# A two-layer graph kernel: the folded value-output product in seven products of 256 cubed, row maxima taken from adj, layernorm sums of two batches on ScalarE, the bias row ahead of the flag

## The chip, the cores and the metric

The kernel runs on one core of a Trainium2 chip. The metric is the device time of one execution in microseconds (us). Three runs of the kernel before took 1082.97, 1084.35 and 1084.44 us; the median is 1084.35.

The engines have short names here, as in the profile: PE is TensorE's matrix multiply and PEld its weight load, DVE is VectorE, ACT is ScalarE, POOL is GpSimd, SP is SyncE, which here only issues transfers. Each engine runs its own list of instructions in order and waits on semaphores for the others.

## What is computed

There are 32 batches of 512 rows with 512 features. Each goes through two layers, both with a layernorm and relu ahead and an addition behind:

```python
h = jnp.maximum(_layernorm(x, axis=-1), 0.0)
x = x + einsum('bnd,do->bno', einsum('nm,bmd->bnd', adj, h), weight) + bias
h = jnp.maximum(_layernorm(x, axis=-1), 0.0)
q, k, v = h @ Wq + bq, h @ Wk + bk, h @ Wv + bv      # 8 heads of 64
scores = q k^T / 8 + (1.0 - adj)[None, None, :, :] * -1e9
x = x + softmax(scores) v @ Wo + bo
```

`adj` is a 512 x 512 matrix of reals between 0 and 1, not of zeros and ones. The term -1e9 (1 - adj) therefore outweighs the scores: in each row the largest adj takes the whole softmax, unless two of them lie too close. The kernel looks for that at run time. It finds the largest adj of each row and the gap to the second, bounds the scores by the sums of squares of Wq and Wk, counts the rows that some row points to, and forms a flag. If the flag says so, attention is a row look-up: out[n] = h[idx[n]] @ (Wv Wo) + (bv Wo + bo). This holds for the given data, and the run takes that path (`single_path`).

## The kernel before

**The opening** (lines 72 to 268) runs once, in an order written out by hand (`tc.manual_schedule`). It loads the weights, adj, the first batches of x, and then does these things on PE, in this order:

- transposes of `wv` into `wvT` (`turn`, L116), four 128 x 128 at a time, and between them the folded product `wvo` = wv x wo (L148): for each of four row blocks four matmuls of 512 columns. ACT copies each result out of PSUM into `wvo` (L167), permuting the columns.
- transposes of adj into `adjT` (L106), which ACT copies out (L110).
- the first matrix product of batch 0, `yT` = h x adjT (L225): four blocks of four matmuls of 512 columns, between which come small matmuls of the flag: `few` (L232), `many` (L218, L219), the bias row bv x Wo (L224) and the flag itself (L221).

DVE meanwhile forms the bias row's parts (`bias_part`, L133 and L135), the row maxima and where they stand (`peaks`, L128 and L129), the statistics of batch 0 and 1 (`Norm.stats`, BN_STATS L319 and aggregate L320; `power` L325 with POOL's L326; `offset` L329), sums of blocks of adjT, w0 and wvo (`sum_a`, `sum_b`, L287 to L305), the decision (L203 to L212), `cvo` (L259) and the flag as an integer (L255). ACT makes `mask` = -1e9 (1 - adj) in two passes a row block (`scale`, L121 and L122), applies the layernorm with relu (`Norm.relu`, L337), squares Wq and Wk (L200) and empties PSUM. All engines then read the flag from memory and branch (L270).

**The rest** (`single_path`) is a loop over batches that interleaves layer 0 of one batch with the preparation of the next and layer 1 of the one before. A matrix product of 512 cubed is done by `product` (L382): seven products of 256 cubed, each four matmuls of 256 columns, with sums of blocks prepared by DVE. The seven pieces have the names p1, p5, u2, c11, c22, c12, c21 and three PSUM banks: p1, u2, c22 and c21 add up in one bank, p5 and c12 in another. So u2 can only start when p1 has been copied out of the bank (L427 on ACT), and so on. Only batch 0's layer product is done in four row blocks with 512 columns (`layer0_rows`, L514).

What the other engines do beside the products is put into numbered steps: `put(batch, step, function)`. Steps 0 to 6 go beside layer 0 of batch b, 7 to 13 beside the aggregation of batch b + 1, 14 to 20 beside layer 1 of batch b - 1. For batch 0 the steps 0 to 3 go beside `layer0_rows` and hold steps 4 to 6 as well. Within a step each engine gets its instructions in the order of the `put` calls. In this first round stand, on DVE: the sums of batch 1's h (`h0_sum`), the additions L517, `number_rows`, the statistics of batch 0's second layernorm (`halves`), and those of batch 2's first (steps 8 to 11).

**The end.** The last batch's rows are gathered by GpSimd (`get_all`, L545), transposed on PE (`transpose_all`, L552) and multiplied with `wvo` (L564). Batch 30's rows are stored (`put_z`, L598), gathered again (`fetch`, L611), added (L616) and stored to the output.

Of the kernel before, what the change touches and what calls it, by code (L numbers as in the profile page):

```python
# [17 lines left out]
P = 128  # L18
# [7 lines left out]
def gnn_two_layers(ctx: ExitStack, tc: tile.TileContext, x, adj, w0, b0, wq, bq, wk, bk, wv, bv, wo, bo, out):  # L26
# [45 lines left out]
    with ExitStack() as tmp, tc.manual_schedule():  # L72
# [3 lines left out]
        adj_s, mask = (look.tile([P, C, N], F32, name=n) for n in ("adj_s", "mask"))  # L76
# [4 lines left out]
        wvT = yT  # L81

# [3 lines left out]
        for i, (t, w, c) in enumerate([(wv_s, wv, 0)] + [(wo_s, wo, c) for c in range(DC)] +  # L86
                                      [(wv_s, wv, c) for c in range(1, DC)]):
            (nc.sync, nc.scalar)[i % 2].dma_start(t[:, c:c + 1, :], rows(w, c, 1))
# [8 lines left out]
        for t, v in ((bv_c, bv), (bt[0], bq), (bt[1], bk)):  # L97
            nc.gpsimd.dma_start(t, v.rearrange("(c p) -> p c", p=P))
        first = look.tile([P, 1], F32, name="first")
        nc.scalar.activation(first, ones[:, 0:1], AF.Relu)  # L100

        def transposed(t, dst):
            pts = [ps_l.tile([P, C, P], F32, name=f"pt{m}") for m in range(C)]
            for c in range(C):
                for m in range(C):
                    nc.tensor.transpose(pts[m][:, c, :], t[:, c, m * P:(m + 1) * P], ident)  # L106
                if c % 2 == 1:
                    yield
            for m in range(C):
                nc.scalar.copy(dst[:, m, :], pts[m].rearrange("p c q -> p (c q)"))  # L110
            yield

        def turn(i):
            pt = ps_l.tile([P, C, P], F32, name=f"pt{i}")
            for j in range(DC):
                nc.tensor.transpose(pt[:, j, :], wv_s[:, i, j * P:(j + 1) * P], ident)  # L116
            (nc.scalar.copy, nc.scalar.copy, nc.vector.tensor_copy, nc.vector.tensor_copy)[i](
                wvT[:, :, i * P:(i + 1) * P], pt)

        def scale(c):  # L120
            nc.scalar.activation(mask[:, c, :], adj_s[:, c, :], AF.Copy, bias=-1.0)  # L121
            nc.scalar.activation(mask[:, c, :], mask[:, c, :], AF.Copy, scale=NEG)  # L122
# [4 lines left out]
        def peaks(c):  # L127
            nc.vector.max(top[:, c, :], mask[:, c, :])  # L128
            nc.vector.tensor_scalar(sel[:, c, :], mask[:, c, :], top[:, c, 0:1], None, op0=ALU.is_equal)  # L129
# [6 lines left out]

        flips = transposed(adj_s, adjT)
        idle = ps_l.tile([P, C, P], F32, name="pt3")
        for i in range(14):
            nc.tensor.transpose(idle[:, i % C, :], ident, ident)  # L140
        turn(0)
        later = {(0, 2): 1, (1, 0): 2, (1, 2): 3}
        for i in range(DC):
            ps = ps_l.tile([P, D], F32, name="mm", bufs=2)
            for j in range(DC):
                if (i, j) in later:
                    turn(later[i, j])
                nc.tensor.matmul(ps, wvT[:, j, i * P:(i + 1) * P], wo_s[:, j, :], start=(j == 0), stop=(j == DC - 1))  # L148
            if i == 0:
                for j in range(DC):  # L150
                    bias_part(j)
            if i == 1:
                next(flips)
                peaks(0)
                peaks(1)
            if i == 2:
                next(flips)
                for n in (0, 1):
                    norms[0].stats(n)
                norms[0].power()  # L160
                for v, r in ((b0, b0_r), (bo, cvo)):
                    nc.gpsimd.dma_start(r, bass.AP(tensor=v.tensor, offset=v.offset, ap=[[0, P], [1, D]]))
                norms[1].stats(0)
                norms[0].offset()
                norms[1].stats(1)
                norms[1].power()
            nc.scalar.copy(wvo[:, i, :].rearrange("p (c q e) -> p q c e", q=4, c=4),  # L167
                           ps.rearrange("p (q c e) -> p q c e", q=4, c=4))
            if i < 2:
                scale(2 * i)  # L170
                scale(2 * i + 1)
            if i == 2:
                next(flips)
                norms[0].relu(0)
                norms[0].relu(1)
                peaks(2)
                norms[1].offset()
                peaks(3)
                norms[1].relu(0)
                norms[1].relu(1)  # L180
# [3 lines left out]
        for c in range(2, C):  # L184
            nc.vector.tensor_add(both, both, sel[:, c, :])
        gap = look.tile([P, C], F32, name="gap")
        nc.vector.tensor_sub(gap, top[:, :, 0], top[:, :, 1])
        least = look.tile([P, 1], F32, name="least")
        nc.vector.tensor_reduce(least, gap, AX.X, ALU.min)
        for i in range(4):  # L190
            sum_b(nc, adjT_s, adjT, i)

        sums = look.tile([P, 4], F32, name="sums")
        few = ps_l.tile([P, 4, C], F32, name="few")
        many = ps_l.tile([P, 4, C], F32, name="many")
# [17 lines left out]

        for d in range(DC):
            ps = ps_l.tile([P, N], F32, name="mm", bufs=2)
            for m in range(C):
                if d == 2 and m == 1:
                    nc.tensor.matmul(many[:, 0, :], ones, used, start=True, stop=True)  # L218
                    nc.tensor.matmul(many[:, 1, :], ones, sums, start=True, stop=True)  # L219
                if d == 3 and m == 2:  # L220
                    nc.tensor.matmul(few[0:1, 1, 0:1], sure, ones[:, 0:1], start=True, stop=True)  # L221
                if d == 3 and m == 0:
# [761 lines left out]
```

## Time and profile before

| | us |
|---|---|
| median of three runs | 1084.35 |
| lowest, highest | 1082.97, 1084.44 |
| the profiled execution | 1083.92 |
| its span, first to last instruction | 1081.7 |
| PE busy in it | 1067.9 |
| opening, until the first product of `layer0_rows` | 43.57 |
| `layer0_rows`, to its end | 57.83 |

The span is what the profile covers; 2.2 us lie around it. TensorE's granted clock was 0.997. A line of the timeline has the start in us, the duration in us, the engine, the line of the code, the operation, what it writes and reads, and in brackets how long the engine had been idle before and what ended that. Consecutive instructions of one kind are drawn together as x4, x8; durations of neighbours overlap a little, so that work is best counted from start to start. In the lists of waits a line reads: who waited, for what, us in total, how often, the longest.

Some more starts from DVE's timeline: the peaks of the first row block at 15.92, the statistics of batch 0 from 18.16, the sums of adjT from 26.70, the statistics of batch 1 from 29.30, the flag at 39.98, the addition of the bias row to `cvo` at 42.64, the four additions of b0 from 44.68, the first sum of batch 1's h at 47.09.

### The profile page before, as it was taken

To read this page: it belongs to the slowest core of one execution; us is meant where nothing else is said; L and a number is where in the kernel's file an instruction comes from. 1 tells how busy PE (TensorE), PEld (TensorE's weight loads), DVE (VectorE), ACT (ScalarE), POOL (GpSimd) and SP (SyncE) were. 2 spreads that over 40 slices of the span, in tenths; PEclk is the share of its full clock that TensorE was granted. 3 is DMA by queue.
4 is the path that set the end of the run, shared out by engine and by line. 5 is a ranking of instruction groups with operands and counts; after the bars stand their busy time and mean duration, and the time that the engine had idled before them with its cause. 6 is when DMAs were issued, how large, how long until landed. Compare 5 with 4: busy or idle time off the path is not lost.

```text
span 1081.7 us, 15914 instructions
## 1 busy us (share of the span) xinstructions
PE 1067.9 (99%) x5418; PEld 941.9 (87%) x5418; DVE 902.8 (83%) x1851; ACT 362.2 (33%) x664; POOL 439.2 (41%) x522
## 2 busy tenths in 40 slices
PE   9999999999999999999999999999999999999996
PEld 5488989999998999998999998999898899999893
DVE  5888888888888888888888988888888888888873
ACT  5324323334422324432323432323332333442331
POOL 2024554333454333454433354433455434355413
PEclk9999999999999999999999999999999999999998
DMA  9144766667767666767666776665766666775638
GB/s 329 40 96 141 183 183 160 160 167 196 187 179 181 151 167 184 196 176 188 150 160 183 201 185 175 160 167 158 207 183 183 146 169 171 196 186 151 148 104 265
DMA packets 162443, 186.90 MB, mean 173 GB/s; under 512 B 15024, under 2 KB 102320, under 8 KB 162352
## 3 DMA queue, kind: packets, MB, share of 16 engines
q1 hardware_dynamic: 132816, 116.89, 37.2%
q0 software_dynamic: 27968, 66.61, 26.8%
q10 hardware_dynamic: 1568, 2.29, 0.6%
q8 instruction: 44, 0.72, 0.3%
q14 instruction: 47, 0.39, 0.1%
HBM read 96.28 MB, written 89.46 MB: 172 GB/s over the span
## 4 chain that ended last, share of the span: by engine, by line
PE 94%; DMA 2%; DVE 1%; POOL 1%; issue 1%; ACT 1%; SPq 0%; POOLq 0%; ACTq 0%; DVEq 0%
PE mm L388 89%; PE mm L148 1%; PE mm L225 1%; PE mm L514 1%; POOL x L602 1%; DMA yT<-z,place 0%; ACT h L337 0%; DMA h<-hs,idx 0%; DMA z<-zr 0%; DMA out_dram<-x 0%; PE pt L140 0%; DMA hs<-h 0%; PE pt L116 0%; DVE st L319 0%; DVE x L616 0%
## 5 line engine op out<-in xcount | busy, mean ns | idle before, releaser
L602 POOL DMA_INDIRECT x<-z,place x116 | 182.7, 1575 | 351.8 <-issue 193.7
L427 ACT COPY yT<-mm 128x512 f32<-128x512 f32 x124 | 71.8, 579 | 542.6 <-PE mm L388 534.6
L445 DVE TENSOR_TENSOR x<-mm,x 128x512 f32<-128x512 f32 x217 | 149.6, 689 | 86.1 <-PE mm L388 86.1
L337 ACT ACTIVATE h<-x,off,rstd 128x512 f32<-128x512 f32 x256 | 194.3, 807 | 52.2 <-DVE off L329 49.9
L326 POOL TENSOR_TENSOR rstd<-ve,mhalf 128x2 f32<-128x2 f32 (+1 forms) x97 | 106.3, 1095 | 233.5 <-DVE ve L325 233.0
L319 DVE BATCH_NORM_STATS2 st<-x 128x6 f32<-128x512 f32 x256 | 171.4, 670 | 1.2
L388 PE MATMUL mm<-adjT_s,h0s 128*128 128x256 f32 x744 | 170.8, 379 | 0.2 <-ACT yT L427 0.2
L388 PE MATMUL mm<-w_t,sel 128*128 128x256 f32 x744 | 170.7, 379 | 0.0
L388 PEld LDWEIGHTS mm<-adjT_s,h0s 128*128 128x128 f32 x744 | 141.2, 190 | 19.9 <-ACT yT L427 0.6
L388 PEld LDWEIGHTS mm<-w_t,sel 128*128 128x128 f32 x744 | 141.3, 190 | 19.3
L526 POOL DMA_INDIRECT hs<-h,dest x124 | 126.7, 1022 | 23.9 <-issue 22.4
L388 PE MATMUL mm<-w_s,yT 128*128 128x256 f32 x496 | 117.2, 379 | 0.0
L388 PE MATMUL mm<-adjT,h 128*128 128x256 f32 x496 | 117.2, 379 | 0.0
L388 PE MATMUL mm<-hTs,wvo_t 128*128 128x168 f32 x720 | 112.4, 306 | 0.0
L438 ACT ACTIVATE zs<-mm,cvo_c 128x168 f32<-128x168 f32 x240 | 83.0, 397 | 75.5 <-PE mm L388 75.5
L388 PEld LDWEIGHTS mm<-adjT,h 128*128 128x128 f32 x496 | 94.2, 190 | 13.2 <-issue 0.5
L388 PEld LDWEIGHTS mm<-hTs,wvo_t 128*128 128x128 f32 x720 | 105.5, 190 | 0.0
L388 PEld LDWEIGHTS mm<-w_s,yT 128*128 128x128 f32 x496 | 92.9, 190 | 11.3
L494 DVE TENSOR_TENSOR x<-x,b_r 128x512 f32<-128x512 f32 x124 | 83.8, 676 | 0.0
L388 PE MATMUL mm<-hT,wvo 128*128 128x168 f32 x480 | 78.2, 306 | 0.0
L388 PEld LDWEIGHTS mm<-hT,wvo 128*128 128x128 f32 x480 | 72.7, 190 | 1.6
L425 DVE TENSOR_TENSOR yT<-mm,yT 128x512 f32<-128x512 f32 x93 | 64.0, 688 | 5.7 <-PE mm L388 1.7
(159 smaller groups left out, 1285.7 us busy)
## 6 DMA issues: line engine op xcount, KB each, us to landing
out_dram<-x SPq DMA_DIRECT2D x124, 256.0 KB
x<-in_x_dram SPq DMA_DIRECT2D x120, 256.0 KB
hc<-hs SPq DMA_DIRECT2D x124, 176.0 KB
z<-zr SPq DMA_DIRECT2D x120, 96.0 KB
z<-zr SPq DMA_DIRECT2D x120, 80.0 KB
hs<-h,dest POOLq DMA_INDIRECT x124, 6.3
x<-z,place POOLq DMA_INDIRECT x116
adj_s<-in_adj_dram SPq DMA_DIRECT2D x2, 512.0 KB
```

Of the source, the lines that this page charges most:

```text
L148: nc.tensor.matmul(ps, wvT[:, j, i * P:(i + 1) * P], wo_s[:, j, :], start=(j == 0), stop=(j == DC - 1))
L319: self.nc.vector.bn_stats(st, self.src[:, self.chunks[i], :])
L326: self.nc.gpsimd.tensor_tensor(self.rstd, ve, self.mhalf[:, 0:n], ALU.pow)
L337: self.nc.scalar.activation(dst, src, AF.Relu, bias=self.off[:, i:i + 1], scale=self.rstd[:, i:i + 1])
L388: nc.tensor.matmul(bank[:, m, 0:half], lhs[:, k, m * P:(m + 1) * P], rhs[:, k, :], start=(first and m == 0 and k == 0), stop=(k == 1), ski ...
L425: nc.vector.tensor_add(dst, bank, dst)
L427: nc.scalar.copy(dst, bank)
L438: nc.scalar.activation(dst[:, m, :], bank[:, m, :], AF.Identity, bias=cvo_c[:, 2 * i + m:2 * i + m + 1])
L445: nc.vector.tensor_add(dst, bank, dst)
L494: nc.vector.tensor_add(X[b][:, c, :], X[b][:, c, :], b0_r)
L526: stored = nc.gpsimd.indirect_dma_start(out=HS[b], out_offset=bass.IndirectOffsetOnAxis(ap=dest[:, i:i + 1], axis=0), in_=H1[b][:, i, :], ...
L602: nc.gpsimd.indirect_dma_start(out=X[b][:, c, :], out_offset=None, in_=Z[b], in_offset=bass.IndirectOffsetOnAxis(ap=place[:, c:c + 1], axi ...
```

## The change

- The folded product is done as `product` does it, in seven products of 256 cubed (`fold`), with sums of blocks of wvT (in `xs[2]`, batch 2's room, as scratch) and of wo (in `wvo_t`, as scratch). The column permutation is now in how wo is read, in runs of 32 elements.
- The loads of wv and wo are cut otherwise: wv's first two row blocks in two column halves, the rest in halves of 512 KB. The rows b0 and bo are loaded at the start on POOL's queue.
- `mask` is gone; the maxima, the comparison and the index search use adj itself, and the first two values of each row are scaled afterwards (`tops`).
- The sums for the first layernorm of batches 1 and 2 are made on ACT, by a copy and a square that accumulate along the row (`NormAct`); batch 2's from steps 2 and 3 instead of 8 to 11.
- The bias row's parts are formed after the peaks; its matmul, and its addition to `cvo`, now come before the flag. Order on DVE around the flag changes with it; yT's last block is copied by ACT alone.
- Two sums of wvo go to batch 0's step 13, none is left in batch 1's step 5. `transpose_all(0)` of the last batch goes from step 18 to 19.

```diff
-        adj_s, mask = (look.tile([P, C, N], F32, name=n) for n in ("adj_s", "mask"))
+        adj_s = look.tile([P, C, N], F32, name="adj_s")
+        wvT_t = xs[2].rearrange("p c (a n) -> p c a n", a=2)
+        wo_t = wvo_t.rearrange("p t c (k n) -> p t c k n", k=2)
-        for i, (t, w, c) in enumerate([(wv_s, wv, 0)] + [(wo_s, wo, c) for c in range(DC)] +
-                                      [(wv_s, wv, c) for c in range(1, DC)]):
-            (nc.sync, nc.scalar)[i % 2].dma_start(t[:, c:c + 1, :], rows(w, c, 1))
+        for h in range(2):
+            nc.sync.dma_start(wv_s[:, 0:2, h * 256:(h + 1) * 256], rows(wv, 0, 2)[:, :, h * 256:(h + 1) * 256])
+            nc.scalar.dma_start(wo_s[:, 2 * h:2 * h + 2, :], rows(wo, 2 * h, 2))
+        nc.sync.dma_start(wv_s[:, 2:4, :], rows(wv, 2, 2))
...
+        for v, r in ((b0, b0_r), (bo, cvo)):
+            nc.gpsimd.dma_start(r, bass.AP(tensor=v.tensor, offset=v.offset, ap=[[0, P], [1, D]]))
...
-        def scale(c):
-            nc.scalar.activation(mask[:, c, :], adj_s[:, c, :], AF.Copy, bias=-1.0)
-            nc.scalar.activation(mask[:, c, :], mask[:, c, :], AF.Copy, scale=NEG)
+        def turn(i, j):
+            pt = corner(2 * i + j)
...
+            nc.scalar.copy(dst[:, 0, :], src[:, 0, :])
+            (nc.vector.tensor_copy if i == 0 and j == 0 else nc.scalar.copy)(dst[:, 1, :], src[:, 1, :])
+        def wo_sum(i):
+            t = [wo_t[:, n].rearrange("p c k (q e) -> p c (k q) e", e=32) for n in range(4)]
+            x1, x2 = ((wo_blk(0, 1), wo_blk(0, 0)), (wo_blk(1, 1), t[0]), (wo_blk(1, 1), wo_blk(0, 1)),
+                      (wo_blk(1, 0), t[1]))[i]
+            nc.vector.tensor_sub(t[i], x1, x2)
+        def fold(ps, lhs, rhs, first):
+            for m in range(2):
+                for k in range(2):
+                    r = rhs[:, :, k, :] if len(rhs.shape) == 4 and rhs.shape[2] == 2 else rhs[:, :, 4 * k:4 * k + 4, :]
...
+                    nc.tensor.matmul(o, lhs[:, k, m * P:(m + 1) * P], r,
+                                     start=(first and m == 0 and k == 0), stop=(k == 1), skip_group_check=True)
...
-            nc.vector.max(top[:, c, :], mask[:, c, :])
-            nc.vector.tensor_scalar(sel[:, c, :], mask[:, c, :], top[:, c, 0:1], None, op0=ALU.is_equal)
+            nc.vector.max(top[:, c, :], adj_s[:, c, :])
+            nc.vector.tensor_scalar(sel[:, c, :], adj_s[:, c, :], top[:, c, 0:1], None, op0=ALU.is_equal)
...
+        turn(0, 0)
+        wo_sum(0)
+        turn(0, 1)
+        u, v, w = (bank(i) for i in (0, 1, 2))
+        fold(u, blk(wvT, 0, 0), wo_blk(0, 0), True)
+        nc.scalar.copy(blk(wvo, 0, 0), u)
+        turn(1, 0)
+        turn(1, 1)
+        fold(w, blk(wvT, 1, 0), wo_blk(1, 0), True)
+        for i in range(1, 4):
+            wo_sum(i)
+        for i in range(3):
+            sum_a(nc, wvT_t, wvT, i)
+        nc.vector.tensor_add(blk(wvo, 0, 0), w, blk(wvo, 0, 0))
+        sum_a(nc, wvT_t, wvT, 3)
+        fold(v, wvT_t[:, 0], wo_t[:, 0], True)
+        nc.scalar.copy(blk(wvo, 1, 1), v)
+        fold(u, wvT_t[:, 1], wo_t[:, 1], False)
+        nc.scalar.copy(blk(wvo, 0, 1), u)
+        peaks(0)
...
+        next(flips)
+        fold(u, wvT_t[:, 2], wo_t[:, 2], False)
+        peaks(1)
+        norms[1].offset()
+        nc.vector.tensor_add(blk(wvo, 1, 1), u, blk(wvo, 1, 1))
+        next(flips)
+        next(flips)
+        fold(v, wvT_t[:, 3], wo_blk(1, 1), False)
...
+        peaks(2)
+        nc.vector.tensor_add(blk(wvo, 0, 1), v, blk(wvo, 0, 1))
+        fold(u, blk(wvT, 1, 1), wo_t[:, 3], False)
+        nc.scalar.copy(blk(wvo, 1, 0), u)
...
+        nc.vector.tensor_scalar(tops, top[:, :, 0:2], 1.0, NEG, op0=ALU.subtract, op1=ALU.mult)
...
+                if d == 2 and m == 3:
+                    nc.tensor.matmul(bias, ones, part, start=True, stop=True)
+                if d == 3 and m == 1:
                     nc.tensor.matmul(few[0:1, 1, 0:1], sure, ones[:, 0:1], start=True, stop=True)
...
-            nc.scalar.copy(yT[:, d, 0:N // 2 if d == 3 else N], ps[:, 0:N // 2 if d == 3 else N])
+            nc.scalar.copy(yT[:, d, :], ps)
...
+            if d == 1:
                 nc.vector.tensor_scalar_min(used, few[:, 0, :], 1.0)
                 if B > 1:
+                    norms.append(NormAct(nc, small, mhalf, xs[1], hs[1], range(C)))
+                    for c in range(C):
+                        norms[2].first(c)
...
             if d == 2:
                 decide()
+                if B > 1:
+                    norms[2].mean()
+                    for c in range(C):
+                        norms[2].second(c)
...
+                nc.vector.tensor_add(cvo, bias, cvo)
         nc.vector.tensor_copy(flag, few[0:1, 1, 0:1])
+        for i in range(2):
+            sum_a(nc, wvo_t, wvo, i)
+        if B > 1:
+            norms[2].power()
+        for c in range(C):
+            nc.vector.tensor_add(xs[0][:, c, :], xs[0][:, c, :], b0_r)
+        if B > 1:
+            norms[2].offset()
+            for c in range(C):
+                norms[2].relu(c)
+        for c in range(C):
+            nc.vector.max_index(idx[:, c, :], top[:, c, :], adj_s[:, c, :])
...
+class NormAct(Norm):
...
+    def row_sum(self, i, kind, to, **more):
+        c = self.chunks[i]
+        self.nc.scalar.activation(self.dst[:, c, :], self.src[:, c, :], kind, accum_out=to[:, i:i + 1], **more)
+    def first(self, i):
+        self.row_sum(i, AF.Copy, self.sum)
+    def mean(self):
+        self.nc.vector.tensor_scalar_mul(self.sum, self.sum, -1.0 / self.src.shape[2])
+    def second(self, i):
+        self.row_sum(i, AF.Square, self.sq, bias=self.sum[:, i:i + 1])
...
+            if b == 0:
+                put(2, 2, lambda b: ahead.append(ln0(b, NormAct)))
+                for c in range(C):
+                    put(2, 2, lambda b, c: ahead[0].first(c), c)
+                put(2, 3, lambda b: ahead[0].mean())
+                for c in range(C):
+                    put(2, 3, lambda b, c: ahead[0].second(c), c)
...
+                    put(0, 13, lambda b, i: sum_a(nc, wvo_t, wvo, i), i)
...
-                put(b, 18, lambda b: transpose_all(0))
+                put(b, 19, lambda b: transpose_all(0))
...
-                put(1, 5, lambda b: sum_a(nc, wvo_t, wvo, 3))
```

## The prediction

> **What bounds the kernel now.** I read the page's busy shares first, then the waits of TensorE (PE), then PE's timeline of the opening, then the other engines beside it.
>
> ```profile
> PE 1067.9 (99%) x5418; PEld 941.9 (87%) x5418; DVE 902.8 (83%) x1851; ACT 362.2 (33%) x664; POOL 439.2 (41%) x522
> ```
>
> PE is busy 1067.9 of 1081.7 us. The steady part, from 58 us on, is PE against PE; only a PE instruction removed or a PE wait removed can shorten the run. The waits of PE over the whole span:
>
> ```profile
> PE mm L514 <- DVE cvo L259: 1.7, 1, 1.7
> PE pt L140 <- POOL ident masks.py:199: 1.4, 1, 1.4
> PE pt L552 <- DMA h<-hs,idx: 1.4, 1, 1.4
> PE mm L148 <- ACT yT L117: 0.7, 1, 0.7
> ```
>
> So there is a wait at the hand-over from the opening to the first layer product (L514), and one near the end (L552). PE's timeline of the opening:
>
> ```profile
> 4.55 1.12 PE L116 MATMUL pt<-ident,x 128*128 128x128 f32 x4
> 6.34 3.78 PE L148 MATMUL mm<-x,yT 128*128 128x512 f32 x4 [0.68 <-ACT yT L117]
> ...
> 22.01 3.60 PE L148 MATMUL mm<-x,yT 128*128 128x512 f32 x8
> 25.45 3.60 PE L225 MATMUL mm<-adjT,h 128*128 128x512 f32 x8
> ...
> 43.57 7.10 PE L514 MATMUL mm<-w_s,yT 128*128 128x512 f32 x16 [1.72 <-DVE cvo L259]
> ...
> 57.83 1.89 PE L388 MATMUL mm<-adjT,h 128*128 128x256 f32 x8
> 59.55 3.62 PE L388 MATMUL mm<-adjT_s,h0s 128*128 128x256 f32 x16
> ```
>
> The timeline shows two records for one matmul. Four 512-wide ones take 25.45 - 22.01 = 3.44 us, 0.86 each; four 256-wide ones 59.55 - 57.83 = 1.72 us, 0.43 each. The first two 512-wide ones took twice that (x4 in 3.78, elsewhere 1.88). Beside them, what ScalarE (ACT) and VectorE (DVE) did where PE enters the steady part:
>
> ```profile
> 58.24 0.13 DVE L329 SCALAR_TENSOR_TENSOR off<-mv,rstd 128x2 f32<-128x2 f32 x1
> ...
> 58.54 1.52 ACT L337 ACTIVATE h<-x,off,rstd 128x512 f32<-128x512 f32 x2 [13.45 <-DVE off L329]
> 59.96 0.56 ACT L427 COPY yT<-mm 128x512 f32<-128x512 f32 x1
> ```
>
> This is the place that decides. The copy at 59.96 empties the first bank of `aggregate(1)` ("p1"), and the third product ("u2") adds into that bank. PE wanted u2 at 59.55 + 1.73 = 61.28; the copy ended at 60.52. The slack is 0.76 us, and behind it stands DVE, which delivers `off` last.
>
> **What the Trainium skill says.** "TensorE: Matmul & The Clock Gate", section "What's actually happening": PE runs at half clock until about 3.4 us of sustained work, and falls back after an idle window of that length. The trace agrees with the first half (records of twice the length until about 10.2 us); no gap here is long enough to show the second. "ScalarE: Activation LUTs", "Rules for kernel authors": about 0.3 us an ACTIVATE with a bias pointer and 0.83 ns an element. The trace has 0.81 us for 512 with two pointers (L337), 0.62 with none (L121). "DMA: Bandwidth & Descriptors", "Queues, rings and completion order": each DMA engine takes turns between its queues, packet by packet, so a load moved forward takes bandwidth from loads beside it. Here the DMA share is about 1.0 from 8 us on.
>
> **The change part by part**, against the profiled execution (1083.92 us, its span 1081.7 and 2.2 around it; the runs' median is 0.43 higher).
>
> *Folded product.* 16 x 0.86 = 13.76 us become 28 x 0.43 = 12.04 us: PE loses 1.72 us. Reading `wo` in runs of 32 elements I price at nothing: DVE L260, which walks the same way, takes 0.69 like any 512-wide pass. DVE gains 8 operand sums and 3 additions from PSUM at a start-to-start of 0.60 to 0.72 us (L299 to L305). Walk: transposes of the first corner end at 5.68 as before; ACT's half 0.37 and DVE's half 0.42 in turn, beside the second corner's transposes; first fold from 6.6, at half clock 4 x 0.85, to 10.0; eight transposes to 10.9; second fold to 12.65. ACT copies the last corner by 11.8, DVE's first sum is ready at 12.5, so the third fold runs 12.65 to 14.4 without a wait, the fourth to 16.1, adjacency transposes to 17.0, fifth fold to 18.7, transposes to 19.6, sixth to 21.3. DVE's list from 11.85: four sums and one addition to 15.0, peaks 1.12, statistics of batch 0 3.9 (18.16 to 22.06 before), peaks 1.13, `off`, then the addition that frees the last fold's bank, to 21.85. PE waits 0.6 us there and starts L225's products at 23.65, against 25.45: 1.8 us gained.
>
> *Bias row and flag.* The `bv` parts (2.85 us, 8.36 to 11.21 before) move on DVE to behind the peaks: DVE reaches `used` at 32.6, PE wants it at 32.2, a wait of 0.45. L225's part ends at about 40.0 (41.87 before). `cvo` is added ahead of the flag, so the hand-over waits only for ACT's full 0.58 us copy of yT: L514's products start at 40.7, against 43.57. Gained so far: 2.85 us. The two row loads now come first on POOL, which was idle from 4.1 to 20.2, 0.6 us each; their 0.5 MB at the 390 GB/s of the DMA view are at most 1.3 us for the weights beside them: 0 to +1.3, taken 0, since PE needs the last wv half only at 10.0.
>
> *Peaks from adj.* Eight ACT passes of 0.63 us go; none is on the path (DVE reached the peaks 0.24 us after the masks). One small DVE operation is added, 0.15.
>
> *Sums of batch 1 on ScalarE.* Four BN_STATS with aggregates (0.82 each, 3.3 us) leave DVE. ACT gets four sums between its yT copies, then four squares after the third copy: at (0.3 + 512 x 0.83 ns) = 0.72 us, an estimate from the ScalarE page and inside 0.62 to 0.81 of the trace, with an accumulator read of 0.09 start-to-start (L200) and an overlap of 0.09, 0.72 each. They run 37.0 to 39.9 and end as L225's part does: no PE cost. But `power` now waits on DVE for them, and behind it stand the four b0 additions (2.4), the row look-ups (2.7), the cvo column (1.3), then the whole list of the first layer product.
>
> *Sums of batch 2 on ScalarE.* DVE restarts at 39.9, has those 6.5 us, then h0 sums, additions, row numbering and statistics as before (47.09 to 58.24, 11.15 with a wait of 1.5 that falls away): `off` and `mean` at 56.2, against 58.24. So DVE gains 2.0 us where PE gained 2.85. ACT's four squares wait for `mean`, and they stand ahead of the two relus and the p1 copy: 56.45 + 4 x 0.72 + 1.42 + 0.56 = 61.3. PE has p1 and p5 done at 40.7 + 14.26 + 3.45 = 58.4 and waits 2.9 us for u2. u2 begins at 61.3, as before: **the opening's whole gain is handed back here, 0.0 us net** (+0.15 for wake-ups). Later the DVE list has caught up (it waits for PE at c11), so nothing more is owed.
>
> *Two wvo_t sums and the last one move* into batch 0's third product, where the products that need sel come 1.7 us apart: 0.
>
> *transpose_all one step later.* Before: the product ahead of it ended at 1054.0, PE waited for rows landing at 1055.4, transposed to 1056.03, then had two products of 1.14. Now one of these fills the wait: everything after is 1.14 us earlier, and the stores of batch 30 that the last gathers wait for as well. At worst the gathers are held by full DMA queues: 0 to 1.5, taken 1.14.
>
> Sum: 0.0 + 0.15 - 1.14 = -1.0 us: 1082.9, or 1083.3 from the median; I put **1082.9**.
>
> **The rivals.**
> (A) As summed; its own range 1081.6 to 1084.6, from squares at 0.62 to 0.81 (4 count after `mean`, 4 before `power`: 8 x 0.1) and the loads' 0 to 1.3.
> (B) The opening's gain survives: DVE reaches `mean` 2 us earlier than my list, because PE warms sooner or the passes pack closer, or ACT clears p1 sooner. For it: the DVE list is a sum of sixty steps. Against: every step's pitch is from the trace. 1083.92 - 1.14 - (1 to 2.85) = 1079.9 to 1081.8, centre 1081.0.
> (C) The wait before u2 grows until the clock falls. Place: PE between p5 and u2. At 0.72 the gap is 2.9 us; with 0.86 or more for a square it passes 3.4 us, and some 3.5 us of matmuls then run at half clock, +1.75 on top of 8 x 0.14 = 1.1, together 1084.8; with 1.0 each, 1086.9. So it is slower from 0.86. For it: the passes write, square, point at a bias and accumulate at once. Against: L200 squares and accumulates at 0.85 ns an element.
> (D) The loads decide: the bias rows delay wv, adj and x by the full 1.3 us and the DVE list with them: 1084.2.
> (E) It isn't what it says: the strided operand halves PE's rate in 12 matmuls, 12 x 0.43 = 5.2 us, part of it before the DVE list: 1087.
>
> **How the numbers follow.** A 0.42, B 0.31, C 0.15, D 0.09, E 0.03. A measurement of this kernel tells about 0.2%, 2.2 us, from no change: below 1082.2 is faster, above 1086.5 slower. Faster: B and 0.06 of A, 0.37. Slower: 0.10 of C and E, 0.13. Same: 0.50. The range 1080.3 to 1086.3 leaves out some 0.06 of B below and 0.13 above.
>
> **What would show it.** L225's product from about 23.6 and the first layer product from about 40.7: the fold and the flag are right. A PE wait of about 2.9 us for the ScalarE copy before u2: the handing back is right; its absence is B. Squares of 0.7 us; records of double length after that gap are C. First-fold records of more than 0.43 us past 12 us are E. At the end PE's wait for rows down from 1.4 to about 0.4. I am wrong if u2 begins before 60 or after 63 us.

## The result, and the profile after

The changed kernel takes 1088.96 us (median of five runs, 1088.29 to 1089.82), the kernel before, on the same chip, 1084.05 (1082.93 to 1084.44): ratio 1.0048, 95% interval [1.0033, 1.0062]. It is slower by about 4.9 us, where 1082.9 was predicted with a range to 1086.3. The profiled execution has a span of 1086.5 us, before 1081.7, at nearly the same granted clock (0.998, before 0.997).

The busy times of the page after:

```profile
PE 1067.3 (98%) x5442; PEld 946.3 (87%) x5442; DVE 901.4 (83%) x1847; ACT 369.8 (34%) x693; POOL 447.0 (41%) x522
```

TensorE (PE) is busy 0.6 us less than before in a span 4.8 us longer. So the new arithmetic, taken together, is not dear; PE waits more. Its list of waits after (who waited, for what, us in total, times, longest):

```profile
PE mm L459 <- ACT yT L498: 2.9, 1, 2.9
PE pt L128 <- DMA x<-in_L_gnn_Wv_dram: 1.5, 3, 0.8
PE pt L172 <- POOL ident masks.py:199: 1.4, 1, 1.4
PE mm L459 <- DVE zs L506: 1.3, 1, 1.3
PE mm L459 <- DVE x L516: 0.9, 1, 0.9
PE mm L585 <- ACT yT L272: 0.7, 1, 0.7
```

Four of these are new: 2.9 for ScalarE's copy of p1, 1.5 for wv's loads, 0.9 for an addition on VectorE (DVE), 1.3 for `zs`. Two are shorter: the hand-over to the first layer product (L585, before L514) waits 0.7 instead of 1.7, and the wait of 1.4 for rows near the end is down to 0.3. PE's timeline of the opening after:

```profile
5.16 1.11 PE L128 MATMUL pt<-ident,x 128*128 128x128 f32 x4 [0.48 <-DMA x<-in_L_gnn_Wv_dram]
7.04 1.11 PE L128 MATMUL pt<-ident,x 128*128 128x128 f32 x4 [0.77 <-DMA x<-in_L_gnn_Wv_dram]
7.95 3.13 PE L152 MATMUL mm<-x,yT 128*128 128x256 f32 x8
11.33 1.09 PE L128 MATMUL pt<-ident,x 128*128 128x128 f32 x8 [0.25 <-DMA x<-in_L_gnn_Wv_dram]
12.26 1.89 PE L152 MATMUL mm<-x,yT 128*128 128x256 f32 x8
...
25.19 5.31 PE L269 MATMUL mm<-adjT,h 128*128 128x512 f32 x12
...
42.78 7.11 PE L585 MATMUL mm<-w_s,yT 128*128 128x512 f32 x16 [0.72 <-ACT yT L272]
```

Three times PE waits for a piece of wv. The first fold starts at 7.95, where 6.6 was walked and the kernel before started its product at 6.34; the first two waits, 0.48 and 0.77, make most of that delay. The operation with adjT (L269, L225 before) starts at 25.19 against 25.45, the first layer product at 42.78 against 43.57: of the 2.85 us expected by then, 0.8 are there. The place where PE enters the steady part, all engines, after:

```profile
57.03 1.89 PE L459 MATMUL mm<-adjT,h 128*128 128x256 f32 x8
58.52 0.16 DVE L398 TENSOR_SCALAR sum<-sum 128x4 f32<-128x4 f32 x1
58.72 0.72 ACT L392 ACTIVATE h<-x,sum 128x512 f32<-128x512 f32 x1 [8.73 <-DVE sum L398]
...
61.56 1.50 ACT L380 ACTIVATE h<-x,off,rstd 128x512 f32<-128x512 f32 x2
62.97 1.04 ACT L498 COPY yT<-mm 128x512 f32<-128x512 f32 x2
63.58 0.70 PE L459 MATMUL mm<-adjT_s,h0s 128*128 128x256 f32 x2 [2.93 <-ACT yT L498]
```

`mean` is formed at 58.52; ScalarE, idle for 8.73 us, makes its four squares in 2.84 us, then two relus, then copies p1 out at 62.97; u2 (the line at 63.58) starts 2.3 us later than before (61.28). Two more starts complete the account: the first piece of layer 0's product is at 72.32 for batch 1 (69.92 before, 2.4 late) and at 107.18 for batch 2 (102.60, 4.6 late); the waits of 0.9 and 1.3 lie between. From there to 1044.6 us (last product with hT, 4.45 late) nothing changes.

### The profile page after: what moved, and what is told of

Read it like the earlier page. It is cut to its first block, busy times and chain, and to the rows that moved or that the text cites. A ratio compares the mean times of both kernels' runs of the same rounds, so it can differ in the third digit from the quotient of the medians.

```text
span 1086.5 us, 15990 instructions
## 1 busy us (share of the span) xinstructions
PE 1067.3 (98%) x5442; PEld 946.3 (87%) x5442; DVE 901.4 (83%) x1847; ACT 369.8 (34%) x693; POOL 447.0 (41%) x522
## 4 chain that ended last, share of the span: by engine, by line
PE 86%; DVE 6%; DMA 3%; POOL 1%; ACT 1%; issue 1%; SPq 1%; POOLq 0%; DVEq 0%; ACTq 0%
PE mm L459 86%; POOL x L673 1%; DMA x<-in_L_gnn_Wv_dram 1%; ACT h L392 1%; DMA yT<-z,place 1%; DVE st L362 1%; DMA z<-zr 1%; ACT h L380 0%; SPq L669 0%; DMA out_dram<-x 0%; DVE x L565 0%; DVE zr L664 0%; DVE yT L496 0%; DMA hc<-hs 0%; POOL rstd L369 0%
## 5 line engine op out<-in xcount | busy, mean ns | idle before, releaser
L516 DVE TENSOR_TENSOR x<-mm,x 128x512 f32<-128x512 f32 x217 | 149.8, 690 | 86.9 <-PE mm L459 86.9
L369 POOL TENSOR_TENSOR rstd<-ve,mhalf 128x2 f32<-128x2 f32 (+1 forms) x95 | 105.0, 1105 | 215.2 <-DVE ve L368 215.2
L362 DVE BATCH_NORM_STATS2 st<-x 128x6 f32<-128x512 f32 x248 | 166.1, 670 | 1.2
L597 POOL DMA_INDIRECT hs<-h,dest x124 | 133.0, 1073 | 25.6 <-issue 22.0
L459 PEld LDWEIGHTS mm<-w_s,yT 128*128 128x128 f32 x496 | 92.9, 190 | 11.3
L496 DVE TENSOR_TENSOR yT<-mm,yT 128x512 f32<-128x512 f32 x93 | 64.0, 688 | 12.1 <-PE mm L459 7.1
```

Source lines behind the costliest of these rows:

```text
L362: self.nc.vector.bn_stats(st, self.src[:, self.chunks[i], :])
L369: self.nc.gpsimd.tensor_tensor(self.rstd, ve, self.mhalf[:, 0:n], ALU.pow)
L459: nc.tensor.matmul(bank[:, m, 0:half], lhs[:, k, m * P:(m + 1) * P], rhs[:, k, :], start=(first and m == 0 and k == 0), stop=(k == 1), ski ...
L496: nc.vector.tensor_add(dst, bank, dst)
L516: nc.vector.tensor_add(dst, bank, dst)
L597: stored = nc.gpsimd.indirect_dma_start(out=HS[b], out_offset=bass.IndirectOffsetOnAxis(ap=dest[:, i:i + 1], axis=0), in_=H1[b][:, i, :], ...
```

## The experiments

The columns are the median, the number of runs and the ratio to the kernel before on the same chip, whose median was 1083.5 to 1083.8. Where two runs on different chips are compared, the ratios are the fairer measure: 0.0010 is 1.08 us.

| run | us | runs | ratio, 95% interval |
|---|---|---|---|
| e1: after, transposes at step 18 again | 1090.41 | 6 | 1.0056 [1.0044, 1.0068] |
| e2: after, batch 2's sums on DVE again | 1085.52 | 19 | 1.0016 [1.0009, 1.0023] |
| e3: after, batch 2's sums a step earlier | 1085.91 | 18 | 1.0018 [1.0011, 1.0025] |
| e4: after, wvo_t sums in batch 1 | 1086.39 | 10 | 1.0028 [1.0019, 1.0037] |
| e5: after, bias rows late | 1087.14 | 6 | 1.0031 [1.0019, 1.0043] |
| e15: after, GpSimd's five loads held back | 1086.79 | 22 | 1.0023 [1.0015, 1.0031] |
| e8: e3 and e4 | 1085.23 | 14 | 1.0015 [1.0005, 1.0025] |
| e7: e8, transposes at step 18 | 1085.63 | 22 | 1.0016 [1.0008, 1.0023] |
| e9: e8, bias rows late | 1083.00 | 22 | 0.9997 [0.9990, 1.0003] |
| e10: e8, GpSimd's five loads held back | 1082.56 | 22 | 0.9989 [0.9982, 0.9997] |
| e11: e10, last halves of wv and wo split | 1081.69 | 11 | 0.9985 [0.9975, 0.9995] |
| e6: before, transposes at step 19 | 1082.88 | 13 | 0.9986 [0.9978, 0.9995] |
| e13: before, bias rows first | 1084.05 | 14 | 1.0003 [0.9993, 1.0013] |
| e14: before, bq's and bk's loads held back | 1083.34 | 14 | 0.9997 [0.9988, 1.0006] |

### The wait before u2

```diff
 e2_dve_sums
-            if b == 0:
-                put(2, 2, lambda b: ahead.append(ln0(b, NormAct)))
...
+            put(b + 2, 8, lambda b: ahead.append(ln0(b)))
+            for c, step in enumerate((9, 10, 13, 13) if b > 0 else (8, 9, 10, 11)):
+                put(b + 2, step, lambda b, c: ahead[0].stats(c), c)
 e3_mean_early (and put ahead of what step 1 and 2 held)
-                    put(2, 2, lambda b, c: ahead[0].first(c), c)
+                    put(2, 1, lambda b, c: ahead[0].first(c), c)
-                put(2, 3, lambda b: ahead[0].mean())
+                put(2, 2, lambda b: ahead[0].mean())
...
-                    put(2, 3, lambda b, c: ahead[0].second(c), c)
+                    put(2, 2, lambda b, c: ahead[0].second(c), c)
```

> The changed kernel with batch 2's first layernorm sums on VectorE again, in steps 8 to 11. Theory Q (the four squares that stand ahead of the p1 copy on ScalarE hold PE): PE's wait of 2.9 us before the third product of the first aggregation shrinks to 0.3 or less, and the run to about 1086.2. Rival L (the late loads have put VectorE's whole list behind, the squares are only in its shadow): the wait stays above 2 us, the run at about 1088.5 or more.

> The changed kernel with batch 2's sums still on ScalarE, but the mean ahead of step 2 on VectorE, so that the squares run where ScalarE sat idle for 8.7 us. Theory Q: the wait before the third product goes to 0.3 or less as in the kernel with the sums on VectorE, about 1086.1. Rival L: the wait stays above 2 us. If this gains nothing while the kernel with the sums on VectorE gains, ScalarE's added work as such costs, not its place.

Both take the wait before u2 away, and both are about 3 us below the changed kernel (1088.96 - 1085.52 = 3.4, - 1085.91 = 3.05). One moves the sums off ScalarE, the other leaves all of them there, one step earlier, with `mean` asked for earlier too. So it is not the squares' work that costs but their place ahead of the p1 copy. PE's timeline of e3:

```profile
11.62 1.97 PE L128 MATMUL pt<-ident,x 128*128 128x128 f32 x8 [2.44 <-DMA x<-in_L_gnn_Wv_dram]
13.38 2.72 PE L152 MATMUL mm<-x,yT 128*128 128x256 f32 x8
...
59.79 3.98 PE L459 MATMUL mm<-adjT_s,h0s 128*128 128x256 f32 x16
```

p5 and u2 run on from 59.79 as one group of 16 records, without a gap. The two lines above show something else: a wait of 2.44 us for wv's last half, and after it matmuls at half clock (2.72 for x8 that took 1.89 elsewhere). That led to the runs on the loads below.

### The wait for the addition on VectorE, and the clock in the gap

```diff
 e4_wvo_later
-                    put(0, 13, lambda b, i: sum_a(nc, wvo_t, wvo, i), i)
+                for i in (2, 3):
+                    put(1, 5, lambda b, i: sum_a(nc, wvo_t, wvo, i), i)
```

> The changed kernel with the two wvo_t sums in batch 1's step 5 instead of batch 0's step 13. Theory W (these two passes of 0.6 us hold back the addition that frees the first bank of batch 1's layer product): PE's wait of 0.9 us on the addition of mm to x goes, about 1088.0. Rival: the wait moves to another product and the run stays at 1088.9.

VectorE's list in the changed kernel has the two sums (L334, L336 on `wvo_t`) ahead of the addition L516 that frees the bank, and PE waits for that addition:

```profile
74.28 0.69 DVE L334 TENSOR_TENSOR wvo_t<-wvo 128x512 f32<-128x512 f32 x1
74.88 0.69 DVE L336 TENSOR_TENSOR wvo_t<-wvo,wvo_t 128x512 f32<-128x512 f32 x1
...
76.09 0.68 DVE L516 TENSOR_TENSOR x<-mm,x 128x512 f32<-128x512 f32 x1
76.82 1.99 PE L459 MATMUL mm<-w_t,sel 128*128 128x256 f32 x8 [0.89 <-DVE x L516]
```

In e4 the wait for `x` is gone. Its worth in time is best read where nothing else gaps: e8 against e3 is 1085.91 - 1085.23 = 0.7 us by the medians, 0.3 by the ratios (PE's wait was 0.9 to 1.3), with intervals that overlap. The wait is shown, its worth isn't resolved. The median of e4 fell by 2.6 us, more than this wait can explain. Its ten runs lie in two groups (1085.96 to 1087.46, and 1089.18 and 1090.73), and the profile, taken of the longest, shows what sets the long ones apart; why the others lie 2.6 us below the changed kernel is not settled. PE's timeline of e4:

```profile
65.04 3.78 PE L459 MATMUL mm<-adjT_s,h0s 128*128 128x256 f32 x8 [2.92 <-ACT yT L498]
68.61 3.06 PE L459 MATMUL mm<-adjT,h 128*128 128x256 f32 x8
```

After the same gap of 2.92 us, u2 and c11 take 3.78 and 3.06 us instead of 1.9 each: the clock fell to half, 3 us more. In the changed kernel's own profile it did not fall. So a gap of 2.9 us is a gamble. How many executions of the changed kernel lose it isn't known, but the mean granted clock of each gives a hint. The five traces with a fall to half have 0.994 to 0.997, the others 0.997 or 0.998. The profiled execution of the changed kernel, its fastest, has 0.998; its other four have 0.995 or 0.996, a level to which only 4 of 176 executions of the kernel before come down. So most of them probably lost clock somewhere, here or in the opening (see the loads below).

### The end

```diff
 e1_end18, e7_three
-                put(b, 19, lambda b: transpose_all(0))
+                put(b, 18, lambda b: transpose_all(0))
 e6_before_end19
-                put(b, 18, lambda b: transpose_all(0))
+                put(b, 19, lambda b: transpose_all(0))
```

> The changed kernel with the last transposes back in step 18. Theory O (the end hangs on the gathers of the last batches, not on PE): PE's wait at the transposes returns to about 1.4 us and PE is 1.1 us later there, but the execution ends within 0.5 us of the changed kernel, about 1088.9. Rival T (PE's step 19 does save 1.1 us and the loss is all elsewhere): about 1090.1.

> The changed kernel with both repairs: batch 2's mean ahead of step 2, and the two wvo_t sums in batch 1's step 5. Theory Q and W (the two waits add): PE has neither the wait of 2.9 us on the copy of p1 nor the one of 0.9 us on the addition to x, about 1085.0 (1.3 less than with the mean moved alone). Rival: only one of them counts, as the second appears elsewhere, about 1086.

> As the kernel with both repairs, and the last transposes back in step 18. Theory O (the end hangs on the gathers): within 0.5 us of the kernel with both repairs. Rival T (step 19 saves what PE shows): 1.1 us more.

> The kernel before, with another part of the change alone: the last batch's transposes one step later (19 instead of 18). Theory O (the end hangs on batch 30's stores and gathers, not on TensorE): TensorE's wait of 1.4 us for rows before the transposes falls to below 0.4, and the span from the last product's start to the end grows by about as much; the time is within 0.5 us of the kernel before. Rival (the prediction's price): 1.1 us faster, 1082.4 where the kernel before has 1083.5.

e8 has neither of the two waits and comes out at 1085.23, near the 1085.0 forecast, though its gain on e3 is smaller than forecast. On the end, e1 is a weak test: it is 1.45 us slower than the changed kernel, with intervals that overlap, and in its profile the clock fell after the gap before u2 (c11 took 3.08). e7 against e8 gives the step 0.4 us, with intervals that overlap too. e6 against the kernel before gives 0.85 by the medians and 1.5 by the ratio, whose interval is 0.5 to 2.4 us. All three point the way of the predicted price of 1.1, which lies inside e6's interval; none settles its size. In the traces PE's wait for rows falls from 1.37 us to 0.19 in e6, as walked. From the start of the last product to the end of the span it is then 1080.2 - 1056.04 = 24.2 us, before 1081.7 - 1058.31 = 23.4: 0.8 of 1.2 goes to the landing of the last gathered rows. In the changed kernel it is 1086.5 - 1061.68 = 24.8, in e8 23.4, with the same code there; e7 and e1, with the old step, have 23.9 and 24.9. So single profiles cannot settle this term. DVE's timeline at the end after:

```profile
1069.80 0.69 DVE L687 TENSOR_TENSOR x<-sel,x 128x512 f32<-128x512 f32 x1 [2.75 <-DMA sel<-z,place]
...
1077.18 0.69 DVE L687 TENSOR_TENSOR x<-yT,x 128x512 f32<-128x512 f32 x1 [2.98 <-DMA yT<-z,place]
```

DVE waits 2.75 and 2.98 us for gathered rows. Where the last additions wait for these, PE being early need not bring its whole lead; that it does not is not shown.

### The loads

```diff
 e5_rows_late, e9_two_rows: to behind norms[0].power(); e13_before_rows_first the other way
-        for v, r in ((b0, b0_r), (bo, cvo)):
-            nc.gpsimd.dma_start(r, bass.AP(tensor=v.tensor, offset=v.offset, ap=[[0, P], [1, D]]))
 e10_two_gated, e15_after_gated (e14_before_gated: behind bv's load)
+        gate = look.tile([P, 1], F32, name="gate")
+        nc.gpsimd.tensor_copy(gate, wv_s[:, 3, 0:1])
         for t, v in ((bv_c, bv), (bt[0], bq), (bt[1], bk)):
```

The copy of one column into `gate` makes GpSimd wait until wv's last row block is there, so that all it issues behind the copy is held back.

> As the kernel with both repairs, and the loads of the rows b0 and bo back behind the first power on GpSimd, as before the change. Theory R (their 0.5 MB at the start delay the weights): the second half of wv lands about 1.3 us earlier, at 10.2 to 10.6 us, and the run is about 1.3 us shorter. Rival S (the many 4-byte elements of bv, bq and bk are what slows the loads): wv lands as late as before, 11.3 to 12.1 us, and the time is the same.

> As the kernel with both repairs, and all five small loads on GpSimd's queue (bv, bq, bk, b0, bo) only once wv has landed. Theory R: as with the rows moved alone. Rival S: only here does wv land earlier, at about 9.5 us, and the run is 1.5 to 2.5 us shorter than with both repairs. If wv lands late here too, the order and size of the weight loads themselves are the cause.

> The kernel before, with one part of the change alone: the two row loads of b0 and bo at the start of GpSimd's queue, behind the three small loads, instead of after the first power. Theory R (the rows take bandwidth from wv and wo, and the start of TensorE is bound by those loads): the second or a later row block of wv lands over 1 us later, TensorE shows a new wait for a DMA of wv or wo of 1 to 2 us before the product of the opening, adjT's product starts at 26.5 to 27.5 instead of 25.45, and the time is 1 to 2 us above the kernel before. Rival (the prediction's price of nothing): the starts and the time are as before, within 0.4 us.

> The changed kernel with the two row loads put back to after the first power, nothing else. Theory R with Q: wv's last half lands by 9 to 10 us and TensorE's wait for it goes, adjT's product starts 0.8 to 1.5 us earlier (about 24), the first layer product at about 41.7, but the wait of about 2.9 us before u2 stays, since ScalarE's list moves with VectorE's; the time is 1 to 2.3 us below the changed kernel, about 1086.5. Rival (the loads matter only together with the other repairs): no gain, 1088 to 1089.

Rows late gain 1085.23 - 1083.00 = 2.2 us on e8 and 1088.96 - 1087.14 = 1.8 on the changed kernel, where the wait before u2 stays at 2.92. The first is clear of noise, the second's intervals overlap, so that the two costs add up is likely and not shown by e5 alone. In e5's profile the wait for the last half is gone, as expected, but L269 starts at 24.88, only 0.3 earlier instead of 0.8 to 1.5. In the landing times, the last wv half arrives 9.9 us after issue in e8 and 8.3 in e9. The row theory fails for the kernel before (e13): the time is 1.0003 of it, PE shows no wait for a load, and L225 starts at 25.14 (its trace has a late clock, in the sense of what follows).

> The changed kernel with all five loads of GpSimd's queue (bv, bq, bk, b0, bo) held until wv has landed, and nothing else. If the loads' cost is its own and adds up with the two waits (u2, x): wv's last half in time without a wait, adjT's product at 22.5 to 24.5, the wait of 2.9 us before u2 and of 0.9 for x stay, and the time is 2.2 to 3.2 us below the changed kernel: 1085.8 to 1086.8, more where the clock falls in the gap. Rival: the gain appears only with the other repairs; then 1088 to 1089.

> The kernel before with bq's and bk's loads held until wv's last row block has landed; bv's stays, since VectorE takes it early. If loads of 4-byte elements slow those beside them whatever the kernel: the rate between 5 and 9 us is above the 273 GB/s of the kernel before, adj and x land earlier, but TensorE, which waits for wv only in executions whose clock rises early (0.5 us there), gains little: 0 to 0.6 us. Rival: the kernel before gains as much as the changed one did from it, over 1 us; then what the repaired version has over the kernel before is due to the loads alone and not to the change.

Holding all five loads gains 2.2 us on the changed kernel, with both PE waits still there (2.92 and 0.88 in its profile), and 2.7 on e8, both clear of noise. Against rows late alone it is 0.4 more, with intervals that overlap. What the profile shows of DMA between 5 and 9 us, first the changed kernel, then e10:

```profile
DMA packets 885, 1.31 MB, mean 329 GB/s; under 512 B 142, under 2 KB 387, under 8 KB 885
```

```profile
DMA packets 882, 1.56 MB, mean 391 GB/s; under 512 B 48, under 2 KB 190, under 8 KB 882
```

As many packets, 0.25 MB more. e15 and e11 have 1.56 MB too. The seven traces with the changed kernel's loads have 1.10 to 1.31, e5 and e9 with the rows late 1.12 and 1.18, the kernel before 1.09. Taking away the rows alone thus did not raise this amount; it rose only where the small loads were held as well. That points to the small loads, but they were never held alone on the changed kernel, and in time the difference isn't resolved. e14 is not conclusive on their cost, since bv's load stayed (1.15 MB); its time is that of the kernel before.

Why do 0.5 MB more in flight cost the changed kernel two microseconds and the kernel before none? Three openings side by side. PE's timeline of e6, whose opening is that of the kernel before:

```profile
6.03 1.98 PE L148 MATMUL mm<-x,yT 128*128 128x512 f32 x4 [0.68 <-ACT yT L117]
8.46 0.66 PE L116 MATMUL pt<-ident,x 128*128 128x128 f32 x4 [0.45 <-DMA x<-in_L_gnn_Wv_dram]
...
23.61 3.60 PE L225 MATMUL mm<-adjT,h 128*128 128x512 f32 x8
```

The same of e7, whose opening is that of the changed kernel:

```profile
7.26 1.89 PE L152 MATMUL mm<-x,yT 128*128 128x256 f32 x8
11.81 1.09 PE L128 MATMUL pt<-ident,x 128*128 128x128 f32 x8 [2.66 <-DMA x<-in_L_gnn_Wv_dram]
12.74 3.58 PE L152 MATMUL mm<-x,yT 128*128 128x256 f32 x8
...
26.61 5.31 PE L269 MATMUL mm<-adjT,h 128*128 128x512 f32 x12
```

And of e10:

```profile
7.09 1.89 PE L154 MATMUL mm<-x,yT 128*128 128x256 f32 x8
8.82 1.04 PE L130 MATMUL pt<-ident,x 128*128 128x128 f32 x8
9.69 1.89 PE L154 MATMUL mm<-x,yT 128*128 128x256 f32 x8
...
22.68 3.60 PE L271 MATMUL mm<-adjT,h 128*128 128x512 f32 x8
```

In each of these three the first product runs at full clock (1.98 and 1.89 us, where the profiles before and after have 3.78 and 3.13). Over the 16 traces the clock was up by the first product in eight (e2, e3, e4, e6, e7, e10, e11, e15) and not until about 10 to 11 us in the others. It is not a property of the kernel: e2 and the changed kernel share their opening. Where the clock is up early, PE wants wv's last half at about 8.8 to 9.5; the changed kernel, which loads it in one piece of 512 KB beside wo, the rows and the small loads, has it at 11.3 to 12.1. PE then waits 2.4 to 2.7 us, and the second fold runs at half clock again (3.58 above). So L269 starts at 26.4 to 26.9 in all four such traces (e2, e3, e4, e7), and at 25.2 to 25.6 with the late clock (after, e1, e8). The kernel before starts it at 23.61 with the early clock (e6) and 25.14 to 25.45 with the late one. By these traces the late landing takes from the changed kernel what an early clock gives. The granted clocks fit that: in e8, eight executions of 14 are at 0.996 or less and take no other time than the six above (medians 1085.2 and 1085.5), while with the rows late (e9) none of 22 is so low. The clock isn't all of it: with a late clock in both, L269 starts at 24.34 in e9 and at 25.62 in e8.

e15 also tests the wait before u2 once more, as its opening no longer waits for the last half. PE's timeline of e15, then that of e6, the kernel before with a clock as early:

```profile
40.19 7.11 PE L587 MATMUL mm<-w_s,yT 128*128 128x512 f32 x16 [0.72 <-ACT yT L274]
54.44 1.89 PE L461 MATMUL mm<-adjT,h 128*128 128x256 f32 x8
60.98 1.99 PE L461 MATMUL mm<-adjT_s,h0s 128*128 128x256 f32 x8 [2.92 <-ACT yT L500]
```

```profile
41.74 7.11 PE L514 MATMUL mm<-w_s,yT 128*128 128x512 f32 x16 [1.71 <-DVE cvo L259]
57.72 3.62 PE L388 MATMUL mm<-adjT_s,h0s 128*128 128x256 f32 x16
```

PE is 1.55 us ahead at the first layer product, waits 2.92, and starts u2 at 60.98, where e6 starts it at 57.72 + 1.73 = 59.45. The wait is 2.92 or 2.93 in all five traces that have it, whether PE comes to p1 at 54.44 (e15) or at 58.51 (e4): `mean` is formed 1.48 us after p1's start in e15 and 1.49 in the changed kernel, so DVE's list moves along with PE's.

> The version with both waits taken away and GpSimd's five small loads held until wv has landed, and in addition the last halves of wv and wo cut into single row blocks, spread over SyncE's and ScalarE's queues, wv ahead of wo. If TensorE's start is still bound by wv's last half (transposes of it at 8.82 with no wait), it starts up to 0.6 us earlier and the time falls by as much, to about 1082.0. If it is bound by TensorE itself there, or if wo's last half now lands too late for the second fold, nothing or a loss of up to 1 us.

e11 and e10 can't be told apart. e11's time came near the forecast, but not in the way forecast: PE's start was 0.3 later than in e10, not earlier. Both are faster than both kernels: 0.11 and 0.15% below the kernel before, with intervals that end below 1. So is e6 (0.14%), which changes one step of the kernel before and nothing else; the runs don't tell these three apart.

## Why the prediction was wrong, step by step

Two steps failed, the loads at the start and the balance of the wait before u2.

- **The loads at the start.** The first step that failed: "0 to +1.3, taken 0, since PE needs the last wv half only at 10.0". Holding them back was worth 1.8 to 2.2 us (e5, e9) for the rows and 2.2 to 2.7 with the small loads (e15, e10). Two things were wrong. The half-clock start of one profile was taken for a property of the kernel; with an early clock the need is at about 9. And the landing was never walked: the last half, one piece of 512 KB, lands 9.9 us after its issue in e8. Rival D had the mechanism, with a price (1.3) that is too low and no clock in it.
- **The folded product itself** was right in its rate: x8 records of 1.89 us at full clock, as of any 256-wide group, so rival E is out. The walk to L269 (23.65, measured 25.19) lost its time at the very start. The first fold was walked from 6.6 and started at 7.95, the second from 10.9 (12.26), the third from 12.65 (14.00). In this profile the waits for the two pieces of wv's first half (0.48 and 0.77) made most of that, the one for the last half 0.25. The second piece was waited for in all twelve traces with wv cut this way, 0.74 to 1.50 us, with the other loads held back too; no term of the prediction has it.
- **Bias row and flag** were right in kind: `used` at 33.95 with a PE wait of 0.18 (0.45 walked), and the hand-over now waits only for ScalarE's copy, 0.72. Its start, 42.78 instead of 40.7, inherits the delay.
- **The wait before u2** had the right size: 2.9 walked, 2.93 measured, squares of 0.71 to 0.72 us walked at 0.72. The second step that failed is its balance, "the opening's whole gain is handed back here, 0.0 us net". PE was to come 2.85 us early and lose just that. In the profile its lead at the hand-over was 0.8, and DVE formed `mean` at 58.52 (56.2 walked); u2 came 2.3 us late. With the loads held back (e15) the lead was 1.55 at a like clock, and u2 came 1.5 late. So the wait is a loss of its own that does not shrink with the lead, and taking it away gave about 3 us (e2, e3). That e15 meets the walk's own times closely (40.19 for 40.7, u2 at 60.98 for 61.3) is partly luck, since the walk counted on a late clock.
- **Rival C** set the clock's fall at a square of 0.86 us, from a gap of 3.4. In e1 and e4 it fell after 2.93 and 2.92 us with squares of 0.71. "TensorE: Matmul & The Clock Gate", section "What's actually happening", in the Trainium skill, gives an idle window of about 3.4 us and says that it is free-running; the prediction took the length as a threshold. These traces show the fall after shorter gaps, and a first rise at anything from about 5 to 11 us. Rival C's sum is also off: 1082.9 + 1.75 + 1.1 is 1085.8, not 1084.8.
- **Two wvo_t sums at 0** was wrong: PE waited 0.89 us for `x` (L516), since in DVE's list the sums stand ahead of the addition that frees the bank for u2 of batch 1's layer product. Without them (e8 against e3) the kernel gained 0.3 to 0.7, which is within the noise.
- **The transposes one step later**, "taken 1.14": the wait fell as walked (1.37 to 0.19 in e6). The time gained is 0.4 in one pair (e7, e8), 0.5 to 2.4 in the other (e6), so 1.14 is neither shown nor refuted. Whether the gathers' landing takes part of it stays open.
- **The wait of 1.3 for `zs`** was in no list. In that execution POOL's power (L369) of four columns took 3.22 us:

```profile
101.03 3.22 POOL L369 TENSOR_TENSOR rstd<-ve,mhalf 128x4 f32<-128x4 f32 x1 [5.76 <-DVE ve L368]
```

  DVE waited for it, and the addition to `zs` stands behind. The power took 3.21 in e15 and in e6 too, the latter with the old code there, and the wait is 1.3 in these three; in the other 13 traces the power took 1.41 and the wait is 0.3 or less. It comes and goes in both kernels, and nothing here shows that the change causes it; it makes about 1 us of the profiled span's 4.8.

The sum over medians, from the changed kernel to e10: 3.05 (squares earlier) + 0.7 (wvo_t) + 2.7 (loads) = 6.4 us, or 1088.96 - 1082.56; these are differences taken one after the other, so they add up by themselves, and each has an uncertainty of some 1 us. By the ratios, which take the chip out, they are 3.3, 0.3 and 2.8. Left is a gain of about 1 us, with the loads held back and both waits gone. That this is near what was predicted for the whole is chance: the prediction gave the opening nothing and the end 1.14, while e10 is already 1.5 us ahead of e6 at u2, at a like clock (57.96 against 59.45).

What stays open: what the small 4-byte loads cost by themselves (0.4 us between e9 and e10, not resolved); whether cutting wv as before would have cured the changed kernel too; and whether adj's loads, which SyncE issues from 2.32 us on instead of 4.69, slow wv as well. None of these was tried alone, and neither were the fold, the maxima from adj, batch 1's sums and the bias row.

## What to carry to other kernels

Walk a load-bound start twice, once with the PE clock rising at its earliest and once at its latest, and compare each need with the landing of the very piece that is needed, not with the queue's mean rate: an edit that hides behind a cold clock in one profile can cost in the next execution. Before giving an idle engine new work, look for what it does next that PE is waiting for; here 2.84 us of squares ahead of a 0.56 us copy cost about 3 us, and one step earlier they left no wait. A PE gap near 3 us should be priced with a chance of half clock behind it.

## What was not expected of the hardware

- After a gap of 2.40 to 2.66 us early in the kernel, PE's clock fell to half again at once or within about 1 us of the gap's end in all four traces that have one (e2, e3, e4, e7); after one of 2.92 to 2.93 us before u2, in two of five (e1, e4, but not after, e5, e15).
- The clock came up at about 5 to 7 us in eight traces and at about 10 to 11 in the other eight; among the seven with the changed kernel's opening it was four and three.
- Three loads of 2 KB in 4-byte elements and two broadcast rows of 256 KB, held back until wv had landed, raised what DMA moved between 5 and 9 us from 1.10 to 1.31 MB (seven traces) to 1.56 (three); without the rows alone it was 1.12 and 1.18.
- The same GpSimd power of 128 x 4 took 1.41 us in 13 traces and 3.21 to 3.22 in three, of both kernels.
